# Routing the last group by token slot and loading expert blocks in two parts

## The chip, the cores and the metric

The kernel is one launch on one NeuronCore of a Trainium2 chip. It is written in Bass with the Tile framework: the source fixes what each engine does, a scheduler in the framework puts the instructions of each engine into one fixed sequence, and from then on every engine works through its own queue in order and waits on semaphores. The metric is the time of an execution on the device, in microseconds (us). The engines are called PE (TensorE), DVE (VectorE), ACT (ScalarE), POOL (GpSimd) and SP (SyncE, which here only issues DMAs).

## What is computed

2048 tokens with 256 features pass through four layers in fp32. Each layer adds a cross attention over a context of 77 positions and then a feed-forward part to the token. The change touches layer 3 alone, which is a multi-head cross attention followed by a mixture of eight experts, of which each token takes one. An expert has room for 320 tokens; tokens that find no room go to a shared overflow expert.

```python
def layer3(x, ...):
    x = x + _L3_xattn_ref(_layernorm(x), ctx_1024, Wq, Wk, Wv, Wo, rel_pos_bias, mask)
    xf = _layernorm(x)
    eid = jnp.argmax(jax.nn.softmax(xf @ router_w + router_b, axis=-1), axis=-1)
    onehot = jax.nn.one_hot(eid, 8)
    rank = jnp.cumsum(onehot, axis=0)[jnp.arange(2048), eid] - 1
    valid = rank < 320
    buf = zeros((8, 320, 256)).at[eid, where(valid, rank, 0)].add(xf * valid)
    h = relu(einsum('ecd,edh->ech', buf, w1) + b1)
    y = einsum('ech,ehd->ecd', h, w2) + b2
    yov = relu(xf @ ow1 + ob1) @ ow2 + ob2
    return x + where(valid, y[eid, rank], yov)
```

## The kernel before

**Tokens.** The tokens lie in SBUF as G = 4 groups of J = 4 slots with 128 tokens each (one per partition). A token's row has ROW = 513 floats: x (columns 0 to 255, `xs`), the normalised x (256 to 511, `xns`) and the token's number. Three helpers normalise a group: `measure` takes the statistics (BATCH_NORM_STATS2 and AGGREGATE on DVE, L147 and L148, for each slot) and rstd (two instructions on POOL, L149 and L150, for the four slots at once); `normalize` (L156, DVE) writes `xns`, a slot at a time; `turned` transposes the group on PE (L175) and copies it out of PSUM by ACT (L179) and DVE (L181). `small_logits` (L194) makes the router's logits, two small matmuls for each slot. The tiles of statistics come from a ring of three buffers, which the attention and the routing share.

**Attention of layer 3** (L862 to L998). Sixteen iterations, one for each slot of each group, run through a software pipeline: in step s, stage k works on iteration s - k. The stages are `ahead` (in a group's first three slots, the next group's `measure`, `normalize` and transposes), `queries` (L910, matmuls into a `pq` tile; rope by DVE and POOL, L769 to L779), `queries_turned` (L929), `scores` (L945, two `psc` tiles; then the softmax: L952, L959, L965, L966 on DVE, L961 on ACT, L967 on POOL), `values` (L980 transposes, L982 and L985 copies, L987 matmuls, L990 the add into x on DVE). The stages `measured`, `logits` and `send` of the routing follow behind; they are wrapped by `after`, which runs them for a group when its last slot is through. `pq`, `psc` and later `ph` share a PSUM ring of two buffers, `pbig`.

**Routing** (L1024 to L1119). `measured` takes a group's statistics, `logits` normalises, transposes and computes the logits (bias added at L1058). `send` turns them into the row of a buffer in DRAM: the largest logit (L224 to L228), the rank of a token among those of its expert (a triangular matmul L1075, a running count over the groups L1076), the overflow's rank in the same way (L1098, L1099), and the target row `to` (L1113). Then POOL issues four indirect DMAs (L1115), one for each slot, which scatter the group's 513-float rows into `buf`. A group's ranks need the counts of the groups before it.

**Experts** (L1121 to L1236). Nine blocks, the overflow block o0 with 512 rows first and then the eight experts with 320 rows each, pass through `load`, `hidden` and `answer`, each a step behind the one before. `load` brings a block's rows from `buf` by DMAs that SP issues (L1128 for the full tiles of 128 rows, L1132 for the last 64 rows), and the bias row b2 (L1134); it transposes the normalised columns on PE (L1140), copies them by ACT and DVE (L1145, L1147), converts the token numbers (L1151) and adds b2 to x on POOL (L1153). `hidden` is the first matmul (L1164, `ph`) with the relu on ACT and DVE in turn, `answer` the second (L1176, `poe`), the add of x on DVE (L1180) and the indirect store of the tokens' results by POOL (L1181). SP also issues the weights of the experts (L1210, L1212) in the same queue.

Of the kernel before, what the change touches and what calls it, by code (L numbers as in the profile page):

```python
# [22 lines left out]
F32 = mybir.dt.float32  # L23
# [5 lines left out]
ALU = mybir.AluOpType  # L29
# [4 lines left out]
P = 128  # L34
D = 256
KC = D // P
NB, S = 2, 1024
NT = NB * S
G, J = 4, 4
GT = P * J  # L40
# [3 lines left out]
E = 8  # L44
# [5 lines left out]
EPS = 1e-5  # L50
# [5 lines left out]
ROW = 2 * D + 1  # L56
# [10 lines left out]
def tile_layers(ctx: ExitStack, tc: tile.TileContext, a: dict, out: bass.AP):  # L67
    nc = tc.nc
# [4 lines left out]
    work = ctx.enter_context(tc.tile_pool(name="work", bufs=2))  # L73
    st = ctx.enter_context(tc.tile_pool(name="st", bufs=3))
# [6 lines left out]
    def pbig(name):  # L81
        return ps2.tile([P, 2, 512], F32, tag="p2", name=name)
# [20 lines left out]
    ident = cst[:, C_ID : C_ID + P]  # L103

    tokens = [xp.tile([P, J, ROW], F32, name=f"x{g}") for g in range(G)]
    xs = [t[:, :, :D] for t in tokens]
    xns = [t[:, :, D : 2 * D] for t in tokens]
# [13 lines left out]
    neghalf = cp.tile([P, J], F32, name="neghalf")  # L121
# [124 lines left out]
    def pipelined(n, *stages):  # L246

        for step in range(n + len(stages) - 1):
            for k, stage in enumerate(stages):
                if 0 <= step - k < n:  # L250
                    stage(step - k)
# [613 lines left out]
    def layer3_attention(route, wq, mb3, kblk, vds):  # L865
        with tc.tile_pool(name="a3", bufs=2) as ap, tc.tile_pool(name="a3c", bufs=1) as c3:
# [8 lines left out]
            for b, vd in enumerate(vds):  # L875
                vw = c3.tile([P, NC3, D], F32, name=f"vw3{b}")
                full = (NC3 - 1) * P
# [4 lines left out]
                vws.append(vw)  # L882
            rel = a["relbias"]
            xnTs, rbs, qTs, ss = {}, {}, {}, {}

            def transpose(g):
                xnTs[g] = turned(g, f"a3{g}")
# [107 lines left out]

            for f in begin:
                f(0)
            pipelined(G * J, ahead, queries, queries_turned, scores, values, *map(after, route))  # L998

    NSLOT = E * CAP
    buf = dp.tile([NSLOT + NT, ROW], F32, name="buf")
# [20 lines left out]
    def layer3_ffn():  # L1024
        rw = cp.tile([P, KC, E], F32, name="rw3")
# [22 lines left out]
        made = {}  # L1048

        def measured(g):  # L1050
            measure(g, f"f3{g}")

        def logits(g):
            n = f"f3{g}"
            normalize(g)
            pl = small_logits(turned(g, n), rw, n)
            made[g] = lg = st.tile([P, J, E], F32, tag="lg", name=f"lg_{n}")
            nc.vector.tensor_tensor(lg, pl, rb.unsqueeze(1).to_broadcast([P, J, E]), ALU.add)  # L1058

        def before(dst, src):  # L1060

# [59 lines left out]
        def experts():  # L1121
            outs = iter(dram_disjoint_views(out, E * 3 + 16))

            def load(n, fp, row0, rows, b2):
                m = -(-rows // P)
                xe = fp.tile([P, 4, ROW], F32, tag="xe", name=f"xe_{n}")
                full = rows // P
                nc.sync.dma_start(  # L1128
                    xe[:, :full], buf[row0 : row0 + full * P, :].rearrange("(m p) d -> p m d", p=P)
                )  # L1130
                if full < m:
                    nc.sync.dma_start(xe[: rows - full * P, full], buf[row0 + full * P : row0 + rows, :])  # L1132
                bt = fp.tile([P, D], F32, tag="b2", name=f"b2_{n}")
                nc.sync.dma_start(bt, b2.partition_broadcast(P))  # L1134
                parts = [(i, min(P, rows - i * P)) for i in range(m)]
                xT = fp.tile([P, KC, GT], F32, tag="xT3", name=f"xT_{n}")
                for c in range(KC):
                    px = pone(f"px_{n}{c}")
                    for i, w in parts:
                        nc.tensor.transpose(  # L1140
                            px[:, i * P : i * P + w], xe[:w, i, D + c * P : D + (c + 1) * P],
                            ident[:w, :w],
                        )
                    if c == 0:
                        nc.scalar.copy(xT[:, c, :rows], px[:, :rows])  # L1145
                    else:
                        nc.vector.tensor_copy(xT[:, c, :rows], px[:, :rows])  # L1147
                to = fp.tile([P, 4], U32, tag="ids", name=f"ids_{n}")
                for lo, hi, w in ((0, full, P), (full, m, rows - full * P)):
                    if lo < hi:  # L1150
                        nc.vector.tensor_copy(to[:w, lo:hi], xe[:w, lo:hi, 2 * D])  # L1151

                        nc.gpsimd.tensor_tensor(  # L1153
                            xe[:w, lo:hi, :D], xe[:w, lo:hi, :D],
                            bt[:w].unsqueeze(1).to_broadcast([w, hi - lo, D]), ALU.add,
                        )
                return xe, xT, to, parts, rows
# [29 lines left out]
            with tc.tile_pool(name="f3", bufs=2) as fp:  # L1187
# [15 lines left out]

                def first(k):
                    if k == 0:
                        made[k] = (ow1, ow2), load("o0", fp, NSLOT, GT, a["L3_ffn_ob2"])
                        return
                    e = k - 1
                    w1 = weight([P, KC, HID], f"w1_{e}")
                    nc.sync.dma_start(w1, a["L3_ffn_w1"][e].rearrange("(c p) n -> p c n", p=P))  # L1210
                    w2 = weight([P, NH, D], f"w2_{e}")
                    nc.sync.dma_start(w2, a["L3_ffn_w2"][e].rearrange("(c p) n -> p c n", p=P))  # L1212
                    made[k] = (w1, w2), load(f"e{e}", fp, e * CAP, CAP, a["L3_ffn_b2"][e])
# [21 lines left out]
                        hT = hidden(f"o{i}", fp, xT, rows, ow1, E)  # L1235
                        answer(f"o{i}", fp, hT, ow2, xe, to, parts)  # L1236

        return (measured, logits, send), experts

    with tc.tile_pool(name="masks", bufs=1) as mp:  # L1240
        mask0 = mp.tile([P, G, J * L], a["mask0"].dtype, name="mask0")
# [117 lines left out]
```

## Time and profile before

| | us |
|---|---|
| three runs | 1182.38, 1182.4, 1190.85 |
| median | 1182.4 |
| the profiled execution | 1185.39 |
| its span | 1183.5 |

| stretch of the span | from | to |
|---|---|---|
| end of layer 2's feed-forward part, last `down` add | | about 726 |
| attention of layer 3, first L910 to last L990 | 723.5 | 931.9 |
| routing of the last group, to the issue of the last scatter | 931.9 | 958.0 |
| first block's DMA issued, first `ph` matmul | 960.9 | 968.9 |
| experts | 968.9 | end |

The groups of instructions of layer 3 that cost most, from the page: L987 on PE 76.9 us in 320 instructions (380 ns each), L1176 90.3 us in 384, L1164 75.4 us in 256, L910 57.9 us in 128; L961 on ACT 67.1 us in 256. The mean clock granted to PE over the span was 0.937 of full speed.

A row of the timeline has the start, the time, the engine, the line, the operation, its output and inputs by their names, shape and count, and in brackets the idle time of the engine before it and what ended it. A clock of 1.00 means full speed.

### The profile page before, as it was taken

To read this page: it belongs to the slowest core of one execution; us is meant where nothing else is said; L and a number is where in the kernel's file an instruction comes from. 1 tells how busy PE (TensorE), PEld (TensorE's weight loads), DVE (VectorE), ACT (ScalarE), POOL (GpSimd) and SP (SyncE) were. 2 spreads that over 40 slices of the span, in tenths; PEclk is the share of its full clock that TensorE was granted. 3 is DMA by queue.
4 is the path that set the end of the run, shared out by engine and by line. 5 is a ranking of instruction groups with operands and counts; after the bars stand their busy time and mean duration, and the time that the engine had idled before them with its cause. 6 is when DMAs were issued, how large, how long until landed. Compare 5 with 4: busy or idle time off the path is not lost. (4 is left out here: it accounts for less than half of the span.)

```text
span 1183.5 us, 13880 instructions
## 1 busy us (share of the span) xinstructions
PE 1053.2 (89%) x4778; PEld 662.2 (56%) x4778; DVE 719.0 (61%) x1850; ACT 361.4 (31%) x1108; POOL 389.9 (33%) x370
## 2 busy tenths in 40 slices
PE   5699989999999879696988999999999649999996
PEld 3255544444455446354654655778788527667664
DVE  6778855775779967758686638767878311212211
ACT  1466620000567622231211010655457101101100
POOL 6443310014334324604040002765676331221221
PEclk9799998999999966698989999999999759999998
DMA  8500037432200012201020014222224120443430
GB/s 260 81 1 2 2 63 133 79 63 30 71 2 1 1 38 92 66 1 35 1 43 1 0 53 158 65 56 53 78 44 115 45 103 28 127 146 121 145 99 13
DMA packets 96951, 74.36 MB, mean 63 GB/s; under 512 B 57650, under 2 KB 84578, under 8 KB 96878
## 3 DMA queue, kind: packets, MB, share of 16 engines
q1 hardware_dynamic: 89582, 57.68, 17.8%
q10 hardware_dynamic: 4800, 9.46, 4.4%
q0 software_dynamic: 2496, 6.31, 1.5%
q8 instruction: 40, 0.66, 0.2%
q14 instruction: 33, 0.27, 0.1%
HBM read 54.83 MB, written 19.64 MB: 63 GB/s over the span
## 5 line engine op out<-in xcount | busy, mean ns | idle before, releaser
L408 ACT ACTIVATE s_a<-psc_a,mx_a 128x77 f32<-128x77 f32 x512 | 121.9, 337 | 63.6 <-DVE mx_a L406 61.4
L415 POOL TENSOR_TENSOR s_a<-s_a,sm_a 128x616 f32<-128x616 f32 x64 | 78.5, 1228 | 129.5 <-DVE sm_a L414 98.6
L537 PE MATMUL pe_f<-ew,xnT_f 128*128 128x512 f32 x256 | 117.2, 608 | 0.0
L1176 PE MATMUL poe_e<-w,hT_e 128*128 128x256 f32 (+1 forms) x384 | 90.3, 386 | 1.1 <-DVE ye_e L1180 1.1
L543 DVE SCALAR_TENSOR_TENSOR x<-pe_f,gate_f,x 128x256 f32<-128x256 f32 x128 | 61.8, 483 | 43.6 <-PE pe_f L537 40.9
L961 ACT ACTIVATE s_a<-s_a,mx_a 128x77 f32<-128x77 f32 x256 | 67.1, 347 | 48.5 <-DVE mx_a L959 48.5
L537 PEld LDWEIGHTS pe_f<-ew,xnT_f 128*128 128x128 f32 x256 | 48.3, 194 | 55.4 <-issue 53.5
L746 PE MATMUL po_f<-down2T,hT_f 128*128 128x256 f32 x256 | 68.2, 414 | 12.2 <-DVE x L753 12.0
L1176 PEld LDWEIGHTS poe_e<-w,hT_e 128*128 128x128 f32 (+1 forms) x384 | 66.0, 175 | 21.4 <-issue 2.4
L987 PE MATMUL po_a<-vw,PT_a 128*128 128x256 f32 (+1 forms) x320 | 76.9, 380 | 0.5 <-ACT PT_a L982 0.5
L1164 PE MATMUL ph_e<-xT_e,w 128*128 128x320 f32 x256 | 75.4, 438 | 0.2
L149 POOL TENSOR_SCALAR rstd_a<-mv_a 128x4 f32<-128x4 f32 x16 | 3.7, 236 | 201.2 <-DVE mv_a L148 199.7
L406 DVE TENSOR_REDUCE mx_a<-psc_a 128x4 f32<-128x308 f32 x128 | 57.8, 464 | 13.8 <-PE psc_a L397 8.2
L746 PEld LDWEIGHTS po_f<-down2T,hT_f 128*128 128x128 f32 x256 | 50.2, 205 | 26.9 <-DVE x L753 18.7
L733 PE MATMUL pgu_f<-xnT_f,gate2T 128*128 128x512 f32 x128 | 62.6, 611 | 2.1 <-DVE hT_f L739 1.9
L753 DVE SCALAR_TENSOR_TENSOR x<-po_f,cw_f,x 128x256 f32<-128x256 f32 x128 | 60.3, 478 | 6.2 <-PE po_f L746 3.7
L446 PE MATMUL pc_a<-PT_a,vblk_a 128*32 128x256 f32 (+1 forms) x512 | 57.9, 397 | 4.4 <-DVE PT_a L441 3.8
L987 PEld LDWEIGHTS po_a<-vw,PT_a 128*128 128x128 f32 (+1 forms) x320 | 57.5, 190 | 7.2 <-ACT PT_a L982 0.7
L733 PE MATMUL pgu_f<-xnT_f,up2T 128*128 128x512 f32 x128 | 60.1, 592 | 0.0
L433 PE MATMUL pPT_a<-cst,s_a 128*128 128x128 f32 (+1 forms) x320 | 56.9, 292 | 3.0 <-ACT PT_a L439 1.6
L1164 PEld LDWEIGHTS ph_e<-xT_e,w 128*128 128x128 f32 x256 | 47.4, 190 | 21.0 <-issue 2.7
L413 DVE TENSOR_REDUCE sm_a<-s_a 128x8 f32<-128x616 f32 x64 | 50.3, 786 | 14.6 <-ACT s_a L408 12.2
(290 smaller groups left out, 1954.5 us busy)
## 6 DMA issues: line engine op xcount, KB each, us to landing
w<-in_L_ffn_w SPq DMA_DIRECT2D x16, 1024.0 KB
rb_a<-in_relbias SPq DMA_DIRECT2D x16, 616.0 KB
buf<-none ACTq DMA_DIRECT2D x12, 769.5 KB
xe_e<-buf SPq DMA_DIRECT2D x8, 513.0 KB
vd<-vo SPq DMA_DIRECT2D x8, 308.0 KB
vw<-vd SPq DMA_DIRECT2D x2, 1152.0 KB
x<-in_x SPq DMA_DIRECT2D x4, 512.0 KB
ew<-in_L_ffn_expert_w SPq DMA_DIRECT2D x4, 512.0 KB
```

What stands on the lines that cost most here:

```text
L408: nc.scalar.activation(s[:, c, 4 * i + h, :], sv[:, h, :], AF.Exp, bias=mx[:, h : h + 1], scale=-1.0,)
L415: nc.gpsimd.tensor_tensor(s[:, c], s[:, c], bc(sm, L), ALU.mult)
L446: nc.tensor.matmul(pc[cols, c, :], vblk[g // 2][: wide(m), c, m, cols], t[: wide(m), m, :], start=(k == 0), stop=(k == 1),)
L537: nc.tensor.matmul(pe[:, i, :], xnT[:, kc, j * P : (j + 1) * P], ew[half][:, kc, i * 512 : (i + 1) * 512], start=(kc == 0), stop=(kc == KC ...
L543: nc.vector.scalar_tensor_tensor(x, pe[:, e // 2, (e % 2) * D : (e % 2) * D + D], gate[:, j, 4 * half + e : 4 * half + e + 1], x, ALU.mult ...
L733: nc.tensor.matmul(pgu[:, i, :], wgu[i][:, kc, e * INTER : (e + 1) * INTER], xnTs[g][:, kc, :], start=(kc == 0), stop=(kc == KC - 1),)
L746: nc.tensor.matmul(po[:, e // 2, (e % 2) * D : (e % 2) * D + D], hTs[g, half][:, e, j * P : (j + 1) * P], wd[:, 4 * half + e, :], start=Tr ...
L753: nc.vector.scalar_tensor_tensor(x, po[:, e // 2, (e % 2) * D : (e % 2) * D + D], cws[g][:, j, ee : ee + 1], x, ALU.mult, ALU.add,)
L961: nc.scalar.activation(sh[:, h, :], sh[:, h, :], AF.Exp, bias=mx[:, h : h + 1], scale=-1.0)
L987: nc.tensor.matmul(po, t[:w, m, :], vws[g // 2][:w, m, :], start=(m == 0), stop=(m == NC3 - 1))
L1164: nc.tensor.matmul(ph[:, h % 2, :rows], w1[:, kc, h * P : (h + 1) * P], xT[:, kc, :rows], start=(kc == 0), stop=(kc == KC - 1),)
L1176: nc.tensor.matmul(po, hT[:, h, i * P : i * P + w], w2[:, h, :], start=(h == 0), stop=(h == NH - 1),)
```

## The change

There are three edits in layer 3.

The first moves the stages of the routing. In groups 0 to 2 `measured` no longer has a stage of its own: it runs in the stage of `values` of the group's last slot, and `logits` and `send` each come one step earlier for it.

The second takes group 3 by slots: behind `values` of each of its slots, the new `slot_logits` takes that slot's statistics, rstd (128x1), normalises it, transposes it into a tile of the `pbig` ring, copies it by ACT, makes its logits in the other half of the same tile and adds the bias. `send` is left as it was for the group as a whole.

The third splits the block DMAs of `load` by columns: the normalised x and the token's number (257 floats) first, then x (256 floats). For the block o0 the first part is issued as four DMAs of 128 rows each. An expert's block so has four DMAs instead of two, o0 has five instead of one.

```diff
@@ layer3_attention
+            measured, logits, slot_logits, send = route
...
-            pipelined(G * J, ahead, queries, queries_turned, scores, values, *map(after, route))
+            def last(it):
+                values(it)
+                if it % J == J - 1 and it // J < G - 1:
+                    measured(it // J)
+
+            def slot_then(it):
+                if it // J == G - 1:
+                    slot_logits(it % J)
+                elif it % J == J - 1:
+                    logits(it // J)
+
+            pipelined(G * J, ahead, queries, queries_turned, scores, last, slot_then, after(send))
@@ layer3_ffn
+        def slot_logits(j):
+            g = G - 1
+            n = f"f3{g}{j}"
+            if j == 0:
+                made[g] = st.tile([P, J, E], F32, tag="lg", name=f"lg_f3{g}")
+                made["xnT"] = work.tile([P, KC, GT], F32, tag="xnT", name=f"xnT_f3{g}")
+            x, xn = xs[g][:, j, :], xns[g][:, j, :]
+            bns = st.tile([P, 6], F32, tag="bns1", name=f"bns_{n}")
+            mv = st.tile([P, 2], F32, tag="mv1", name=f"mv_{n}")
+            rstd = st.tile([P, 1], F32, tag="rstd1", name=f"rstd_{n}")
+            nc.vector.bn_stats(bns, x)
+            nc.vector.bn_aggr(mv, bns)
+            nc.gpsimd.tensor_scalar(rstd, mv[:, 1:2], EPS, None, ALU.add)
+            nc.gpsimd.tensor_tensor(rstd, rstd, neghalf[:, :1], ALU.pow)
+            nc.vector.tensor_scalar(xn, x, mv[:, 0:1], rstd, ALU.subtract, ALU.mult)
+            pt = pbig(f"pxs_{n}")
+            for c in range(KC):
+                nc.tensor.transpose(
+                    pt[:, 0, c * P : (c + 1) * P], xn[:, c * P : (c + 1) * P], ident
+                )
+            xnT = made["xnT"][:, :, j * P : (j + 1) * P]
+            nc.scalar.copy(xnT, pt[:, 0, : KC * P].rearrange("p (c q) -> p c q", q=P))
+            for kc in range(KC):
+                nc.tensor.matmul(
+                    pt[:, 1, :E], xnT[:, kc, :], rw[:, kc, :],
+                    start=(kc == 0), stop=(kc == KC - 1),
+                )
+            nc.vector.tensor_tensor(made[g][:, j, :], pt[:, 1, :E], rb, ALU.add)
@@ experts
-            def load(n, fp, row0, rows, b2):
+            def load(n, fp, row0, rows, b2, first=False):
...
-                nc.sync.dma_start(
-                    xe[:, :full], buf[row0 : row0 + full * P, :].rearrange("(m p) d -> p m d", p=P)
-                )
-                if full < m:
-                    nc.sync.dma_start(xe[: rows - full * P, full], buf[row0 + full * P : row0 + rows, :])
+
+                for cols, step in ((slice(D, ROW), 1 if first else 4), (slice(0, D), 4)):
+                    for i in range(0, full, step):
+                        r = slice(row0 + i * P, row0 + min(full, i + step) * P)
+                        nc.sync.dma_start(
+                            xe[:, i : min(full, i + step), cols],
+                            buf[r, cols].rearrange("(m p) d -> p m d", p=P),
+                        )
+                    if full < m:
+                        nc.sync.dma_start(
+                            xe[: rows - full * P, full, cols],
+                            buf[row0 + full * P : row0 + rows, cols],
+                        )
...
-                        made[k] = (ow1, ow2), load("o0", fp, NSLOT, GT, a["L3_ffn_ob2"])
+                        made[k] = (ow1, ow2), load("o0", fp, NSLOT, GT, a["L3_ffn_ob2"], True)
```

## The prediction

> **What bounds the kernel now**
>
> I read the page first (busy shares, then the forty slices), then the timeline of the region that the change touches (700 to 1180 us), then busy time by window, then TensorE's row of the expert loop beside SyncE's.
>
> ```profile
> PE 1053.2 (89%) x4778; PEld 662.2 (56%) x4778; DVE 719.0 (61%) x1850; ACT 361.4 (31%) x1108; POOL 389.9 (33%) x370
> ...
> PE   5699989999999879696988999999999649999996
> ```
>
> TensorE is busy 89% of the span; in the slices of layer 3 (from about 740 us) it stands at nine tenths but for the slices at 915 to 976 us. The windows say what they are:
>
> ```profile
> 735.00:931.90 196.90, 191.72 (x1068) 154.62 (x1068) 146.43 (x312) 107.39 (x342) 124.73 (x95) 1.00 0.27 67
> 931.90:966.60 34.70, 8.72 (x34) 7.30 (x34) 6.42 (x32) 0.58 (x1) 10.46 (x16) 0.54 0.30 108
> 966.60:1180.00 213.40, 197.07 (x792) 138.49 (x792) 40.40 (x90) 23.60 (x45) 43.95 (x45) 0.97 0.30 97
> ```
>
> The columns are length, busy PE, PEld, DVE, ACT, POOL, clock, DMA share, GB/s. The attention is TensorE's (191.7 of 196.9). Between it and the experts lie 34.7 us in which no engine is busy for even a third: a serial chain, and the largest hole in layer 3. In order:
>
> ```profile
> 931.46 0.42 DVE L990 TENSOR_TENSOR x<-x,po_a 128x256 f32<-128x256 f32 x1 [2.52 <-PE po_a L987]
> ...
> 936.75 0.96 POOL L1115 DMA_INDIRECT buf<-x,to_f  x1 [0.30 <-issue]
> 937.74 0.25 POOL L149 TENSOR_SCALAR rstd_f<-mv_f 128x4 f32<-128x4 f32 x1
> 938.07 1.04 POOL L150 TENSOR_TENSOR rstd_f<-rstd_f,neghalf 128x4 f32<-128x4 f32 x1
> 939.15 1.38 DVE L156 TENSOR_SCALAR x<-x,mv_f,rstd_f 128x256 f32<-128x256 f32 x4 [6.50 <-POOL rstd_f L150]
> ...
> 943.64 3.58 PE L194 MATMUL pl_f<-rw,xnT_f 128*128 128x8 f32 x16 [0.78 <-DVE xnT_f L181]
> 947.26 0.19 DVE L1058 TENSOR_TENSOR lg_f<-pl_f,r_L_ffn_router_b 128x32 f32<-128x32 f32 x1 [3.68 <-PE pl_f L194]
> ...
> 953.06 1.12 POOL L1115 DMA_INDIRECT buf<-x,to_f  x1 [1.36 <-DVE to_f L1113]
> ...
> 960.90 0.38 SPq L1128 DMA_DIRECT2D xe_o<-buf  x1
> ...
> 966.70 1.94 PE L1140 MATMUL px_o<-cst,xe_o 128*128 128x128 f32 x8 [13.48 <-DMA xe_o<-buf]
> ```
>
> From the last residual add (end 931.88) to the last group's first scatter 21.2 us pass: POOL does group 2's four scatters first (to 937.7), then rstd, normalise, transposes, 16 router matmuls at a halved clock, and 5.8 us of `send` from the logits to the scatter. Then 7.8 us to the first load's issue, 5.8 us to its landing, 2.2 us to the first `ph` matmul (968.85).
>
> In the expert loop TensorE waits for each block; two of the seven rows:
>
> ```profile
> 1028.35 0.66 PE L1140 MATMUL px_e<-cst,xe_e 128*128 128x128 f32 x4 [1.51 <-DMA xe_e<-buf]
> ...
> 1053.16 0.63 PE L1140 MATMUL px_e<-cst,xe_e 128*128 128x128 f32 x4 [2.22 <-DMA xe_e<-buf]
> ```
>
> The seven idle times (timeline of TensorE, 1007 to 1143 us) are 0.44, 1.51, 2.22, 0.63, 1.90, 0.46, 1.84: 9.0 us.
>
> **The change, part by part**
>
> All against the profiled execution (1185.39 us, span 1183.5), 3.0 above the median 1182.4.
>
> *A. Start of attention 3.* By the compiled order, group 3's measure and normalise leave the end of layer 2's FFN and the attention's start: the three-buffer ring of statistics turns differently. Gone from there are four BATCH_NORM_STATS2/AGGREGATE pairs (0.60 each, between `down` adds that TensorE waits 0.15 to 0.19 us for, in a cycle of 4.33 us) and one normalise of 3.40 us (729.54 to 732.94) in front of the second rope (732.86). TensorE then waits in 735 to 740 us (1.05 us on POOL at 737.75, 0.51 and 0.23 on DVE r_a), and the next `pq` starts at 740.22. With the ropes 3.4 us earlier these waits go: 1.8, and some 0.3 from the `down` cycle. **-2.1**; bounds -2.6 (all) and -0.5 (only the `down` cycle, other queues catch up).
>
> *B. Middle of the attention.* The same 2.4 us of statistics and 1.4 us of normalise (0.35 each, the row at 939.15) reappear on DVE, and 1.3 us (L149 and L150) on POOL, at iterations 4 to 6. DVE is busy 146.4 of 196.9 us there, TensorE's idle rows are only 1.96, 0.63 and 0.29 us. Cover: DVE's free quarter. Bounds: 0 (all hidden) and +3.8 (all on the path); the windows put it near 0. **+1.0**.
>
> *C. Last group by slot.* TensorE's work is the same in count (8 transposes, 8 small matmul pairs), but slots 0 to 2 go between attention matmuls at full clock, and only slot 3's remain behind the last add. New waits, from the compiled order: the slot's tile comes from the two-buffer PSUM ring that `pq` and `psc` use, so iteration 15's second `psc` half stands behind slot 0's bias add, on DVE behind slot 1's normalise, which waits for POOL's rstd. Queued behind it on TensorE is `values`(14), behind that `values`(15), for which POOL's scaling (L967) and all else wait. I walked TensorE through the tail with the row durations: an added stall of 1.2 us near 910, the scaled softmax of iteration 15 at about 930.6 instead of 920.6, last `po` at 936.3 instead of 931.4. On POOL group 2's four scatters (0.96 and 0.30 each, 5 us, now about 930.7 to 935.6) stand before slot 2's rstd; on DVE slot 2's normalise stands before the last add. So that add ends near 937.5, **5.6 us later than today**. Behind it: statistics 0.6, rstd 1.4, normalise 0.4, two transposes 0.6, ACT copy 0.45, four matmul rows 0.9 (0.22 each, as at 943.64), add 0.25, together 4.6; then `send` 5.8: scatter at 947.9 against 953.06. **-5.2**; bounds -7 (no tail stall) and 0 (tail stall twice as long).
>
> *D. First block in parts.* Today 1026 KB land 5.76 us after issue, the next 513 KB 1.66 us later: 317 GB/s, so 1026 KB take 3.3 us and 2.45 are fixed, and the fixed part of the second lay beside the first. Four pieces of 128 KB, issued 0.45 apart (the issues at 960.90 and 961.33), last issue +1.35, last landing about +4.2 (1.35 + 2.45 + 0.4). All but two transposes are done by then; +0.45 and a copy of 0.6 give the first `ph` at +5.3 instead of +7.95. **-2.65**. Against this speaks the Trainium skill, page "DMA: Bandwidth & Descriptors", section "Measured (HBM→SBUF, 128 partitions, SWDGE, issued from GpSimd)": "Batch DMAs to ≥1 MiB for ≥75% of peak. Transfers under 64 KB are descriptor-dominated." Its table has 0.95 us for 64 KB and 6.15 for 1 MB; four pieces of 128 KB, read between (an estimate, 1.3 each) and put one after the other, take 5.2 us: -0.9 instead of -2.65, and the whole sum -12.1 instead of -13.8. I take the row, since it shows two transfers from this buffer overlapping. Bounds -3 and 0.
>
> *E. Experts in parts.* The transposes need only the normalised half and the id: 257 KB instead of 513 before the wait ends, 257 KB / 317 GB/s = 0.83 us earlier. Against the seven waits: 0.44 + 0.83 + 0.83 + 0.63 + 0.83 + 0.46 + 0.83 = **-4.85**. Rows become 1 KB long. The trace has 1-KB rows: a 1-MB w2 load ahead of the block moves its landing from 4.26 us after issue (1002.87 to 1007.13) to 6.9 (1091.83 to 1098.76), 2.67 us per MB, no slower. Bounds -9.0 (waits vanish) and +1 (fixed cost decides, and one more issue of 0.47 ahead in the queue). Costed at nothing: two more issues on SyncE per expert (0.94 us; b2 and w go out that much later, but w1 issued at 1011.52 is first used after 1033); POOL's bias add (L1153) waits for the second part, but its consumer `answer` comes a whole `hidden` (some 20 us) later.
>
> *The `send` of groups 0 to 2 a stage earlier*: 24 small DVE rows near 0.2 us each; they move within the attention, under TensorE's cover: 0, at most +1 where a scatter (5 us of POOL per group) delays an L967.
>
> Sum: -2.1 + 1.0 - 5.2 - 2.65 - 4.85 = -13.8; 1171.6 on the profile's own time, **1168.6 against the median**.
>
> **Rivals**
>
> *1. The split brings nothing in the loop.* If the wait is latency (2.45 of the 4.26 us are fixed) and not bytes, E is about 0 and D is -0.9: -7.2, **1175**. For it: the fixed part is the larger one. Against: landings spread by bytes (1.66 us for 513 KB).
>
> *2. The attention does not start earlier, and its middle pays.* A -0.5, B +3.8: -9.4, **1173**. For: layer 2's cycle is TensorE's own anyway. Against: the 1.05 us wait at 737.75 is on a POOL rope that waited for DVE.
>
> *3. Slower: the in-order tail.* Each slot's transposes wait on TensorE for their normalise, with the attention's matmuls queued behind them, while the tile holds half of the ring. The round trip add, statistics, rstd behind an L967 (1.2), normalise, transposes, copy, matmuls, add is 4.6 to 5 us; four slots uncovered and 5 us of scatters make 25 us, 19.4 more than C has: +5.6, **1188**. For: the compiled order has these waits. Against: the order puts other matmuls (16 to 20 `po` of 3.6 to 4.5 us) between most of them. It decides from the point where the last residual add ends later than 951 us (937.5 + 13.8); below that the kernel is faster.
>
> *That it doesn't do what it says* is excluded by the order: the moves are there.
>
> **How the numbers follow**
>
> Forecast 0.55, rival 1 0.22, rival 2 0.13, rival 3 0.10. A measurement here tells from no change about 1%, 11.8 us: faster means below 1170.6, slower above 1194.2. The forecast's own spread (D, E and C have bounds of 2 to 5 us each, about 4 together) puts 0.7 of it below 1170.6: 0.39; of the rivals 1 and 2, whose terms can also come out larger, 0.13. Faster 0.52. Rival 3 reaches 1194 in half its cases with D and E also lost: 0.06. The rest, 0.42, lies within 1%. The range leaves out rival 3's upper part and a tenth at the low end (all terms at their better bounds would be 1158): 1160 to 1182.
>
> **What would show it**
>
> A: the first `pq` after the first scores near 738, the L156 of 3.40 us gone from 729. C: the last L990 near 935 (937.5 less A and B), one L1115 group ahead of it, the last group's first scatter 10 us behind. D: first px_o transposes 4 us or less after the issue, `ph` 5.3 after it. E: px_e waits of 0 to 1.4 us, together about 4. Wrong: px_e waits as today (rival 1), TensorE's busy share of the attention below 95% before 900 us (rival 2), or an L990 beyond 951 (rival 3).

## The result, and the profile after

The changed kernel takes 1179.1 us (median of 15 runs, 1172.23 to 1185.37) beside 1187.07 us for the kernel before in the same series (15 runs, 1182.24 to 1192.16): ratio 0.9933, 95% interval 0.991 to 0.9956. That is 8 us, 0.7%, where 13.8 us were forecast. Its profiled execution took 1182.58 us with a span of 1180.8.

The layers before layer 3 have the same instructions in both kernels, and yet their gate matmuls end at 706.1 us in the profile before and at 710.1 in the profile after; over all runs of this study that point lies between 704.4 and 715.1. The forecast is therefore checked by stretches that begin after it. Each is the difference of two times in the timeline of TensorE, DVE, POOL or SyncE, in one profiled execution of each kernel.

| stretch, us | before | after | difference | forecast |
|---|---|---|---|---|
| end of layer 2's gate matmuls to the fourth slot's first `pq` (before: 740.22) | 34.13 | 31.89 | -2.24 | A -2.1 |
| from there to the transposes that wait for POOL in group 3 (before: 902.13) | 161.91 | 167.99 | +6.08 | B +1.0, send 0 |
| from there to the last group's first scatter | 50.93 | 43.81 | -7.12 | C -5.2 |
| first scatter to the issue of the first load | 7.84 | 8.28 | +0.44 | 0 |
| first load to the first `ph` | 7.95 | 5.24 | -2.71 | D -2.65 |
| first `ph` to expert 0's first `ph` | 25.39 | 26.45 | +1.06 | 0 |
| from there to the last `poe` | 179.89 | 177.56 | -2.33 | E -4.85 |
| sum | 468.04 | 461.22 | -6.82 | -13.8 |

First the kernel after in windows from the fourth slot's `pq` to the last add, from there to the first block's transposes, and the experts. The columns are the same as before: length, busy PE, PEld, DVE, ACT, POOL, clock, DMA share, GB/s.

```profile
742.00:943.70 201.70, 191.59 (x1060) 152.92 (x1058) 154.75 (x325) 105.85 (x340) 129.29 (x106) 1.00 0.27 66
943.70:964.30 20.60, 5.09 (x22) 4.11 (x21) 4.78 (x27) 0.74 (x2) 5.92 (x12) 0.54 0.23 77
964.30:1177.00 212.70, 196.98 (x792) 137.00 (x792) 39.86 (x90) 23.57 (x45) 43.94 (x45) 0.97 0.33 103
```

The hole between attention and experts is 14 us shorter (20.6 for 34.7). But the attention is longer, and TensorE is idle for 10.1 of its 201.7 us, where it was idle for 3.5 of 191.7 before. So part of the gain is paid back ahead of the hole. The chain through the hole, from the timeline after:

```profile
941.03 0.96 POOL L1157 DMA_INDIRECT buf<-x,to_f  x1 [0.30 <-issue]
...
943.29 0.42 DVE L991 TENSOR_TENSOR x<-x,po_a 128x256 f32<-128x256 f32 x1
...
945.37 0.41 DVE L1087 TENSOR_SCALAR x<-x,mv_f,rstd_f 128x256 f32<-128x256 f32 x1
...
948.11 0.17 DVE L1100 TENSOR_TENSOR lg_f<-pxs_f,r_L_ffn_router_b 128x8 f32<-128x8 f32 x1 [2.33 <-PE pxs_f L1096]
...
953.81 1.12 POOL L1157 DMA_INDIRECT buf<-x,to_f  x1 [1.36 <-DVE to_f L1155]
...
962.09 2.23 SPq L1174 DMA_DIRECT2D xe_o<-buf  x5
964.28 0.29 PEld L1190 LDWEIGHTS px_o<-cst,xe_o 128*128 128x128 f32 x2 [10.40 <-issue]
964.31 1.63 PE L1190 MATMUL px_o<-cst,xe_o 128*128 128x128 f32 x6 [10.34 <-DMA xe_o<-buf]
```

Group 2's scatters now end before the last add, and behind it only one slot is routed: 10.1 us from the end of the add to the first scatter, where 21.2 were needed. The first block's transposes begin 2.2 us after the first issue, for 5.8 before. In the expert loop (TensorE after) the waits are not gone:

```profile
1026.79 0.66 PE L1190 MATMUL px_e<-cst,xe_e 128*128 128x128 f32 x4 [1.78 <-DMA xe_e<-buf]
...
1064.46 5.89 PE L1214 MATMUL ph_e<-xT_e,w 128*128 128x320 f32 x20
1071.63 0.66 PE L1190 MATMUL px_e<-cst,xe_e 128*128 128x128 f32 x4 [1.28 <-DMA xe_e<-buf]
```

They sum to 8.8 us, for 9.0 before. The next rows come from the middle of the attention after, where the 6 us are lost. They show two of the places where TensorE waits for DVE, with the DVE and POOL rows ahead of them.

```profile
820.01 2.35 POOL L779 TENSOR_TENSOR q_a<-q_a,r_a 128x1024 f32<-128x1024 f32 x1 [0.94 <-DVE sm_a L967]
820.35 2.06 DVE L225 TENSOR_TENSOR hot_f<-lg_f,lmx_f 128x32 f32<-128x32 f32 x1
...
824.33 0.28 PE L1117 MATMUL pr_f<-tot_f,cst 128*128 128x8 f32 x1 [0.89 <-DVE tot_f L1115]
...
838.30 2.38 DVE L1148 SCALAR_TENSOR_TENSOR os_f<-os_f,pov_f,o_f 128x4 f32<-128x4 f32 x1
838.32 2.34 POOL L779 TENSOR_TENSOR q_a<-q_a,r_a 128x1024 f32<-128x1024 f32 x1
...
840.73 0.44 PE L175 MATMUL pxnT_a<-cst,x 128*128 128x128 f32 x2 [1.73 <-DVE os_f L1148]
```

Instructions on four or 32 numbers per partition, which take about 0.2 us in the tail, take 2.1 and 2.4 us here, and both end within 0.05 us of POOL's rope addition that runs beside them. The kernel before has the same long rows, in its own order:

```profile
815.64 2.35 POOL L779 TENSOR_TENSOR q_a<-q_a,r_a 128x1024 f32<-128x1024 f32 x1
815.99 2.05 DVE L225 TENSOR_TENSOR hot_f<-lg_f,lmx_f 128x32 f32<-128x32 f32 x1
...
819.69 0.20 DVE L1073 TENSOR_REDUCE tot_f<-hot_f 128x8 f32<-128x32 f32 x1
...
832.58 0.28 PE L1075 MATMUL pr_f<-tot_f,cst 128*128 128x8 f32 x2
...
843.02 2.39 DVE L1106 SCALAR_TENSOR_TENSOR os_f<-os_f,pov_f,o_f 128x4 f32<-128x4 f32 x1
```

Between the two points of the table's second row, the 42 DVE rows of the routing last 16.0 us in sum before and 17.9 after, so the long rows are hardly new. What is new is who waits. TensorE took the counts `tot_f` 12.7 us after they were ready before, and at once after. TensorE has the same 864 instructions there in both kernels. Of the 6.1 us, 4.7 are more idle time, and 1.4 are longer rows, for which no cause was found. Ahead of the wait at its end the stretch has five waits of over half a microsecond after, of 0.84, 0.89, 1.50, 1.73 and 1.53 us, where there was one of 1.96 before. The second and the fourth of them are the two shown; the first stands behind the normalise of 4.88 us (803.59), and the 1.50 and 1.53 are for ACT's copies of the transposed weights of the softmax (`PT_a`). By the starts of the `pq`, the kernel after is 0.2 us late at the tenth and 5.9 at the twelfth and at the last. So nearly the whole loss lies beside group 0's routing, and next to none beside group 1's.

### The profile page after: what moved, and what is told of

It is laid out like the page before. It is cut to its first block, busy times and chain, and to the rows that moved or that the text cites. A ratio compares the mean times of both kernels' runs of the same rounds, so it can differ in the third digit from the quotient of the medians.

```text
span 1180.8 us, 13922 instructions
## 1 busy us (share of the span) xinstructions
PE 1058.2 (90%) x4778; PEld 664.2 (56%) x4778; DVE 722.2 (61%) x1852; ACT 362.7 (31%) x1111; POOL 391.8 (33%) x376
## 5 line engine op out<-in xcount | busy, mean ns | idle before, releaser
L746 PEld LDWEIGHTS po_f<-down2T,hT_f 128*128 128x128 f32 x256 | 50.4, 206 | 26.5 <-DVE x L753 18.3
L1056 ACT ACTIVATE hT_e<-ph_e,b1c 128x320 f32<-128x320 f32 (+1 forms) x36 | 19.6, 545 | 136.6 <-PE ph_e L1214 136.6
L1058 DVE TENSOR_SCALAR hT_e<-ph_e,b1c 128x320 f32<-128x320 f32 (+1 forms) x36 | 20.6, 573 | 64.8 <-PE ph_e L1214 64.8
L739 DVE TENSOR_TENSOR hT_f<-sg_f,pgu_f 128x512 f32<-128x512 f32 x32 | 22.0, 686 | 61.8 <-ACT sg_f L738 61.8
```

The source lines that it names most:

```text
L746: nc.tensor.matmul(po[:, e // 2, (e % 2) * D : (e % 2) * D + D], hTs[g, half][:, e, j * P : (j + 1) * P], wd[:, 4 * half + e, :], start=Tr ...
```

## The experiments

All ratios are against the kernel before, run on the same chip in the same series. Where a text speaks of the third `pq`, the point meant is the fourth slot's first `pq`, from which 161.9 us pass before and 168.0 after to the transposes that wait for POOL. In the table the stretches are those from above: routing is from the end of layer 2's gate matmuls to the last group's first scatter.

| run | ratio (95%) | to fourth `pq` | `pq` to POOL's wait | to scatter (routing) | load to `ph` | `ph` to e0 | experts |
|---|---|---|---|---|---|---|---|
| before | 1 | 34.1 | 161.9 | 247.0 | 7.95 | 25.4 | 179.9 |
| after | 0.9933 | 31.9 | 168.0 | 243.7 | 5.24 | 26.5 | 177.6 |
| e1 split only | 0.9945 (0.9922 to 0.9968) | 34.1 | 162.3 | 247.4 | 5.31 | 26.2 | 176.9 |
| e2 routing only | 0.9966 (0.9943 to 0.9989) | 31.9 | 167.0 | 242.5 | 7.92 | 25.7 | 180.7 |
| e3 slots late | 0.993 (0.9908 to 0.9953) | 34.1 | 161.9 | 248.7 | 4.74 | 25.6 | 177.7 |
| e4 xe three buffers | 0.9875 (0.9824 to 0.9926) | 31.9 | 168.4 | 244.0 | 5.49 | 25.5 | 173.3 |
| e5 ring of four | 0.989 (0.9857 to 0.9923) | 31.9 | 168.0 | 243.7 | 5.15 | 26.7 | 176.3 |
| e6 mixed | 0.9888 (0.9853 to 0.9923) | 34.1 | 162.6 | 240.6 | 5.43 | 26.3 | 177.0 |
| e8 mixed, xe three | 0.9844 (0.9808 to 0.9879) | 34.1 | 162.0 | 240.0 | 5.18 | 26.7 | 173.3 |
| e9 statistics early | 0.9853 (0.9809 to 0.9897) | 31.9 | 162.8 | 237.8 | 5.27 | 26.0 | 173.3 |

### The two halves alone: e1 and e2

e1 is the kernel before with the new `load` only, e2 the changed kernel with the old `load` (L1128 to L1132 as before).

> Only the block DMAs in two parts, on the kernel before; routing as before. By the account of the two traces (first block -1.65 us after 1.06 us of colder matmuls, experts -2.3 us) this run is 4 us faster than the kernel before (ratio 0.9966), the seven waits of the expert transposes still sum to about 8.8 us, and the first ph comes about 5.2 us after the first load's issue. By the prediction's own terms D and E it would be 7.5 us faster (0.9937) with waits of about 4 us in sum.

> Only the routing edits, block DMAs as before. By the account of the two traces (attention start -2.2, its middle +6.1, from there to the last group's first scatter -7.1) this run is about 3 us faster than the kernel before (ratio 0.9973). By the prediction (A -2.1, B +1.0, C -5.2) it would be 6.3 us faster (0.9947). The first scatter of the last group comes about 213.6 us after the first scores' third pq matmul, before 212.8.

The split alone gives 6.5 us by the runs (between the two expectations, and its interval holds both), and 3.5 by the stretches of its one profile; the waits of the transposes sum to 8.0 us and the first `ph` comes 5.3 us after the first load. The routing alone gives 4.0 us, between 3 and 6.3 as well; its first scatter comes 210.6 us after the fourth slot's `pq` (212.8 before), 3 us earlier than the account gave. Both halves gain, and the loss in the middle (167.0) belongs to the routing.

### Which part of the routing costs the middle: e3, e5, e6, e9

e3 puts the stages of groups 0 to 2 back:

```diff
-            pipelined(G * J, ahead, queries, queries_turned, scores, last, slot_then, after(send))
+            def measure_then(it):
+                if it // J == G - 1:
+                    slot_logits(it % J)
+                elif it % J == J - 1:
+                    measured(it // J)
+            def logits_then(it):
+                if it % J == J - 1 and it // J < G - 1:
+                    logits(it // J)
+            pipelined(G * J, ahead, queries, queries_turned, scores, values, measure_then, logits_then, after(send))
```

> The changed kernel with the stages of groups 0 to 2 put back as before (measured, logits and send each a stage later); the last group still goes by slots and blocks still load in two parts. If the moved stages of groups 0 to 2 cause the 6 us lost in the attention's middle, these come back, the gain of 2.2 us at its start goes, and the run is about 11 us faster than the kernel before (ratio 0.991). If the loss comes from the slots themselves (their statistics, rstd and tiles), the ratio stays at 0.9933 or gets worse by the lost start (0.995), and the middle still loses 4 to 6 us.

The middle is as before (161.9), so the slots do not cost it; the moved stages do. But the forecast gain of 11 us was a miss: with group 2 routed late, its `send` and scatters fall beside the slots, and POOL's wait to the first scatter takes 52.6 us instead of 43.8. The early stage is needed for group 2.

e5 was to test the prediction's reason for the moved normalise, the ring of statistics (the tiles mv and rstd likewise, and the tile sel in two buffers to make room):

```diff
-        stats = st.tile([P, J, 6], F32, tag=f"bns{kind}", name=f"bns_{name}")
+        stats = st.tile([P, J, 6], F32, tag=f"bns{kind}", name=f"bns_{name}", bufs=3 if kind else 4)
...
```

> The changed kernel with four buffers instead of three for the statistics that attention and routing share (and two instead of three for the tile sel, to make room), so that group 3's statistics and its normalise go back to the end of layer 2. If the turned ring is what loses time in the attention's middle, the loss of 6.1 us there falls to 1 to 2 us, the gain of 2.2 us at the start goes, and the run is 2 us faster than the changed kernel (0.9915). If it is the earlier logits and send of groups 0 and 1, whose short DVE instructions are held up, only the stall of 0.84 us behind the normalise goes, 4 to 5 us stay lost, and the run is equal to the changed kernel or up to 2 us slower (0.994 or more).

All stretches of the routing are those of the changed kernel to 0.1 us, the stall of 0.83 us behind the normalise among them. So the number of buffers in the ring is not the reason. (Its ratio is better than the changed kernel's, but the intervals overlap, and in the stretches only the experts differ, by 1.3 us.)

e6 routes group 2 in the new stages, and groups 0 and 1 in the old ones (statistics in the next stage, logits and send one later each):

```diff
             def last(it):
                 values(it)
-                if it % J == J - 1 and it // J < G - 1:
+                if it % J == J - 1 and it // J == G - 2:
                     measured(it // J)
...
```

> The changed kernel with groups 0 and 1 routed in the stages of the kernel before, and only group 2 a stage earlier; the last group by slots, blocks in parts. If the earlier stages of groups 0 and 1 cost the middle, the POOL wait of the transposes at 168 us after the third pq comes back to 162 us as before, the tail stays as short as in the changed kernel (43.8 us from there to the last group's first scatter), and the run is about 4 us faster than the changed kernel although the start's 2.2 us are gone (0.990 against the kernel before). If the short tail of the changed kernel needs the early stages of all groups, the tail is longer by 5 us or more and nothing is gained (0.994).

It came out as the first theory said: 162.6, then 43.8 us to the first scatter, and a ratio of 0.9888. The stalls behind `tot_f` and `os_f` are gone. The early routing of groups 0 and 1 costs the middle.

e9 is the same with three buffers for `xe` (see e8), and only the statistics of groups 0 and 1 early.

```diff
-                if early(it):
+                if early(it) or late(it):
                     measured(it // J)
...
```

> The kernel of e8_mixed_xe3, but with the statistics of groups 0 and 1 taken in the stage of their last values as in the changed kernel; their logits and send stay in the stages of the kernel before. If taking group 0's statistics earlier is what moves group 3's statistics and normalise out of the start, the first pq of the fourth slot comes 31.9 us after the end of layer 2's gate matmuls (34.1 in e8), the stall of 0.84 us behind the long normalise is back near 68 us, and the stalls at 82 and 99 us (0.89 and 1.73) are absent; the run is 1 to 2 us faster than e8 (0.983). If the earlier logits and send did that, start and middle are as in e8 (0.9844).

The start is that of the changed kernel (31.9), a stall of 0.77 us behind the long normalise is back at 67.9 us, and the stalls at 82 and 99 us are absent. So the early statistics bring term A, at a price below 1 us, and the early `logits` and `send` of groups 0 and 1 cost 5.2 us (168.0 against 162.8). The time of the run is not told apart from e8's (0.9853 against 0.9844, each with 0.4% on either side); the 2 us stand in the stretches only.

### Why short DVE instructions got long: e7 and e10

Behind the experts of the changed kernel, DVE forms run alone and beside an addition of two 128x1024 tensors on POOL (the code is e10's, shortened):

```diff
+        for k in range(8):
+            nc.scalar.copy(pa, pc)
+            if k % 2:
+                nc.gpsimd.tensor_tensor(pd, pa, pc, ALU.add)
+            nc.vector.tensor_reduce(pm, pa[:, :512], AX.X, ALU.add)
+            if k // 2 == 0:
+                nc.vector.scalar_tensor_tensor(s3[:, :32], s1[:, :32], pm[:, 0:1], s2[:, :32], ALU.add, ALU.mult)
+            elif k // 2 == 1:
+                nc.vector.scalar_tensor_tensor(s3[:, :32], pq[:, :32], pm[:, 0:1], s2[:, :32], ALU.add, ALU.mult)
...
```

> The changed kernel with a measurement of single instructions behind it: each DVE form once alone and once while POOL adds two 128x1024 tensors in SBUF (2.4 us). If DVE is held up where both of its inputs lie in SBUF, or where a tensor_scalar reads and writes SBUF, the 128x32 product of two SBUF tensors takes 0.2 us alone and 1.5 us or more beside POOL, ending with POOL's instruction, and so does the tensor_scalar from SBUF; the product with one input in PSUM, the tensor_scalar from PSUM, the reduction and the statistics take the same in both cases. If the long rows are only waits of the profile for other reasons (data, the queue), all forms take the same in both cases. The time of the run itself is some 20 us longer than the changed kernel.

> As e7_port, with the two-tensor forms made to follow the reduction, so that they begin while POOL's addition runs. If DVE is held up where both tensor inputs lie in SBUF, the scalar_tensor_tensor and the tensor_tensor on 128x32 take 0.2 us alone and about 1.5 us beside POOL, ending with POOL's instruction; the same two forms with one input in PSUM take 0.2 us in both cases. If two inputs in SBUF make no difference, all stay at 0.2 us.

In e7 the two-tensor products ran before POOL began, so that run left them open; e10 answers it. Timeline of e10 (pb_s and pb_t lie in SBUF, pb_p in PSUM), first alone, then beside POOL, then the same form with PSUM beside POOL:

```profile
1173.11 0.25 DVE L1356 SCALAR_TENSOR_TENSOR pb_u<-pb_s,pb_m,pb_t 128x32 f32<-128x32 f32 x1
...
1174.84 2.34 POOL L1353 TENSOR_TENSOR pb_d<-pb_a,pb_c 128x1024 f32<-128x1024 f32 x1 [3.14 <-ACT pb_a L1351]
1175.44 1.78 DVE L1356 SCALAR_TENSOR_TENSOR pb_u<-pb_s,pb_m,pb_t 128x32 f32<-128x32 f32 x1
...
1181.11 2.34 POOL L1353 TENSOR_TENSOR pb_d<-pb_a,pb_c 128x1024 f32<-128x1024 f32 x1 [3.93 <-ACT pb_a L1351]
1181.72 0.25 DVE L1360 SCALAR_TENSOR_TENSOR pb_u<-pb_p,pb_m,pb_t 128x32 f32<-128x32 f32 x1
```

The second row ends at 1177.22, POOL's at 1177.18. With a PSUM input nothing is added. The tensor_tensor goes from 0.19 to 1.77 us, and stays at 0.19 with PSUM. The form of the normalise, timeline of e7:

```profile
1192.19 0.35 DVE L1360 TENSOR_SCALAR pb_u<-pb_s,pb_m 128x256 f32<-128x256 f32 x1
...
1194.01 2.34 POOL L1353 TENSOR_TENSOR pb_d<-pb_a,pb_c 128x1024 f32<-128x1024 f32 x1 [3.85 <-ACT pb_a L1351]
1194.62 1.88 DVE L1360 TENSOR_SCALAR pb_u<-pb_s,pb_m 128x256 f32<-128x256 f32 x1
```

From PSUM it takes 0.48 in both cases, a reduction of 32 numbers 0.18 and the statistics 0.42. This is what the Trainium skill says on its page "SBUF — State Buffer", section "Who interferes with whom": a DVE instruction with two SBUF inputs, or in the two-port mode that a tensor_scalar can enter, and a GpSimd instruction that reads SBUF exclude each other for the whole instruction. The trace agrees to 0.1 us.

A held row need not cost anything, though. In e9 the row of L1148 (there L1166) is held as long, but TensorE works on:

```profile
850.45 2.40 DVE L1166 SCALAR_TENSOR_TENSOR os_f<-os_f,pov_f,o_f 128x4 f32<-128x4 f32 x1
850.45 2.37 POOL L779 TENSOR_TENSOR q_a<-q_a,r_a 128x1024 f32<-128x1024 f32 x1
851.87 0.60 PE L930 MATMUL pqT_a3t<-cst,q_a 128*128 128x128 f32 x4
```

In the changed kernel the transposes `pxnT_a` of the next group stand right behind it, and they take the single PSUM buffer (`pside`) that `pov_f` holds until L1148 has read it.

### What the expert loop waits for: e4 and e8

```diff
-                xe = fp.tile([P, 4, ROW], F32, tag="xe", name=f"xe_{n}")
+                xe = fp.tile([P, 4, ROW], F32, tag="xe", name=f"xe_{n}", bufs=3)
```

> The changed kernel with three buffers instead of two for the tile xe of a block, so that a block's load no longer waits for the answers of the block two before. If the wait of the expert transposes is a matter of when the load can be issued, the seven waits (8.8 us) go to under 1 us and the run is 8 us faster than the changed kernel (0.9865 against the kernel before). If it is a matter of transfer or of the fixed cost of DMAs, they stay and the ratio is 0.992 or more.

> The kernel of the run e6_mixed with three buffers for the tile xe as in e4_xe3. If the two gains lie in different stages and add up, it is 4 us faster than e4_xe3 and about 8 us faster than e6_mixed (0.984 against the kernel before); if they overlap, it is no better than e4_xe3 (0.9875).

All waits of the transposes are gone, and from expert 0's first `ph` to the end TensorE is busy for 173.1 of 173.3 us. With two buffers a load is issued only when the answers of the block two before have been added. The stretch is 4.3 us shorter, not 8.8: TensorE is busy for 4.9 us more there with the same 705 instructions. In the trace it goes over from `ph` to `poe` 45 times instead of 25, most transposes stand 0.20 us apart instead of 0.11, and more `poe` rows 0.31 instead of 0.22; why the pace changes with the order stays open. The ratio goes from 0.9933 to 0.9875, but the two intervals overlap, so the gain is shown by the stretch. With the routing of e6 (e8) both gains add up in the stretches.

The stretch of the experts holds one more thing than waits. In the profile before, the granted clock is 0.50 for 3.41 us (1053.91 to 1057.33), right behind the longest of the seven waits, 2.22 us. The first of these two rows lies there, the second, of the same form, at a clock of 1.00:

```profile
1053.62 5.31 PE L1176 MATMUL poe_e<-w,hT_e 128*128 128x256 f32 x16
...
1099.22 3.62 PE L1176 MATMUL poe_e<-w,hT_e 128*128 128x256 f32 x16
```

That is 1.7 us. e2, with the old `load`, has such a stretch as well (1057.29 to 1060.70), behind a wait of 2.32 us, and no run with the split has one. Whether the shorter waits prevent it was not tested.

### The clock behind the hole: e11 to e15

e11 adds 18 matmuls that nobody reads to e8; e12 has 9 on e9 (its edit is shown). e13 and e14 are e9 without and with the 9, and expert 0's transposes behind the first eight `ph` matmuls. The profile has two rows for each of these matmuls, so that is behind sixteen rows; in e9 itself they stand behind eight rows, and not before the `ph`, as the text of e13 has it. e15 is e14 with expert 0's number conversion behind the first block's copy on DVE.

```diff
+                wt = fp.tile([P, P], F32, tag="warm", name="warm", bufs=1)
+                nc.vector.tensor_scalar(wt, ident, over[:, 0:1], None, ALU.mult)
+                pw = pbig("pwarm")
+                for i in range(9):
+                    nc.tensor.matmul(pw[:, i % 2], wt, ow1[:, 0, :512], start=True, stop=True)
```

> The kernel of e8_mixed_xe3 with 18 matmuls of 128x512 that nobody reads on TensorE between the last count and the first block's transposes, while it would wait for the scatter and the load. If the slow first ph matmuls (6.4 us for eight instead of 3.6) come from the clock after the idle stretch, the stretch from the first ph to expert 0's first falls from 26.7 us to about 24.4 and the run is 2 us faster than e8 (0.9827). If they wait for something else, it stays at 26.7 (0.9844); if the matmuls hold up the first transposes, it gets longer.

> The kernel of e9_measure_early with 9 unread matmuls instead of the 18 of e11_warm, so that they end before the first block lands: in e11 they ran 18.2 us and held up the first transposes by 7 us, while the stretch behind them was 3.1 us shorter. If the clock is what made the first ph matmuls slow, the transposes start 2.2 to 2.6 us after the first load's issue as in e8, the stretch from the first ph to expert 0's first is about 23.5 us instead of 26, and the run is 3 to 4 us faster than e9 (0.982 against the kernel before). If the gain of e11's short stretch came only from the blocks having landed meanwhile, it stays at 26 and the ratio at 0.985.

> The kernel of e9_measure_early with expert 0's block transposes queued on TensorE behind the first eight ph matmuls of the overflow block, where the changed kernel has them, instead of before them. No unread matmuls. The stretch from the last group's first scatter to the first ph falls by about 0.3 us; the first eight ph still run at half clock (about 6.3 us) and the run is equal to e9 within 1 us (0.985).

> e13_order with the 9 unread matmuls of e12_best. If the clock after the idle stretch is what step D lost, the first eight ph take about 3.7 us instead of 6.3, first ph to expert 0's first is about 23.5 us instead of 26, and the time from the first scatter to expert 0's first is about 3 us shorter than in e13_order (ratio about 0.982). If the first ph are slow for another reason (the late DVE half of the copy, their PSUM tile), both stretches are as in e13_order.

> e14_order_warm with expert 0's token numbers converted on DVE behind the overflow block's copy, as in e13_order; in e14 they stood before it and held the second ph matmuls up by 3.4 us. Now only the 9 unread matmuls differ from e13_order. If the clock is what step D lost, the stretch from the first ph to expert 0's first is about 23.5 to 24.5 us (26.9 in e13_order) and the run is 2 to 3 us faster than e13_order (0.981). If not, it is equal to e13_order (0.983).

e11: ratio 0.9859 (0.9814 to 0.9903). The matmuls ran 18.2 us and held the first transposes up by 7 us, and the stretch behind was 23.5 us. e12: 0.9855 (0.9821 to 0.989), inconclusive: TensorE waited 3.2 us for expert 0's transposes ahead of the first `ph`, and the clock fell again (0.50 at 966 to 970 us). e14: 0.9884 (0.9849 to 0.9919), spoilt by a DVE order that held the `ph` up for 3.4 us. In the order around the first `ph`, e13 and e15 differ in the unread matmuls alone. TensorE in e13, without:

```profile
959.48 2.05 PE L1209 MATMUL px_o<-cst,xe_o 128*128 128x128 f32 x8 [10.54 <-DMA xe_o<-buf]
962.03 9.90 PE L1233 MATMUL ph_e<-xT_o,ow 128*128 128x512 f32 x16 [0.51 <-ACT xT_o L1214]
```

and in e15, with:

```profile
952.07 10.35 PE L1273 MATMUL pwarm<-ow,warm 128*128 128x512 f32 x18
962.76 1.84 PE L1209 MATMUL px_o<-cst,xe_o 128*128 128x128 f32 x8 [0.34 <-DMA xe_o<-buf]
965.21 7.32 PE L1236 MATMUL ph_e<-xT_o,ow 128*128 128x512 f32 x16 [0.61 <-ACT xT_o L1214]
```

The same sixteen rows take 7.3 us instead of 9.9; the granted clock is 0.56 in e13's first 6 us of `ph` and 1.00 in e15's. First `ph` to expert 0 takes 24.3 us instead of 26.9. In the runs e13 has 0.9833 (0.9792 to 0.9873) and e15 0.9839 (0.9803 to 0.9876): the 2.6 us of the profile can't be told at this spread. The fastest versions found are e8, e9, e11, e12, e13 and e15 (0.983 to 0.986, with intervals that overlap); their order stays open.

## Why the prediction was right or wrong

- **The serial hole as the place of the gain: right.** C was forecast at -5.2 and is -7.1. The last add came 4.0 us later in its own stretch, for 5.6 forecast, and the add to the scatter fell from 21.2 to 10.1 us, for 10.4 forecast. The feared wait of `psc` and the scatters cost less than walked.
- **A: right in size (-2.2 for -2.1), wrong in its reason.** Not the number of buffers in the ring (e5) but the place of groups 0 and 1's statistics brings it (e9).
- **B and "the `send` of groups 0 to 2 a stage earlier: 0, at most +1": the step that failed.** The middle lost 6.1 us. The prediction said "24 small DVE rows near 0.2 us each; they move within the attention, under TensorE's cover". By e9 against the changed kernel the early logits and `send` of groups 0 and 1 account for 5.2 us of it; the early statistics cost 0.8 (e9 against e8). Two things were missed. A row of 0.2 us lasts up to 2.4 where POOL adds two SBUF tensors beside it (e10), and the kernel before showed such rows already (L225, 2.05 us at 815.99, and L1106, 2.39 us at 843.02). And TensorE's cover ended: these rows lasted about as long before, but in the changed kernel TensorE's queue had the counts and the next group's transposes right behind them. Term B priced group 3's normalise at 0.35 us a slot, though the row of 3.40 us that term A counted was the same normalise; it came back at 4.9 us for four slots. The stalls that the trace puts right behind held rows of the routing, 0.89 and 1.73 us, are half of the 5.2; how the rest divides between held rows and the mere place of the work was not separated.
- **D: the term was right at its place (-2.71 for -2.65), and part was given back behind it.** The granted clock is 0.50 until 971.99 us before and until 972.70 after, and the first `ph` begins at 968.85 before and at 967.33 after. So the `ph` run at half the clock for 3.1 us before and for 5.4 after; 2.2 us more at half the pace are 1.1 us, an estimate from these times, beside the 1.06 that the stretch lost. e15 against e13 shows that this clock is worth 2.6 us of the stretch where all of it is removed. The prediction took the matmuls behind the landing at an unchanged length. It was right to trust the row against the rule that it weighed: four pieces of 128 KB did not take their time one after the other. The first transposes began 2.2 us after the first issue, and those of the last piece 4.05 us after it, for 4.2 forecast.
- **E: mis-sized, -2.3 for -4.85, and what came is not what was forecast.** The forecast was for the waits of the transposes, and they fell by 0.2 us in sum. Blocks that were waited for in both kernels landed 0.2 to 0.9 us sooner after their issue, 0.5 in the mean of six, for 0.83 worked out from bytes. But the sum subtracted that from waits of a fixed order. The order after has the transposes of three blocks behind 20 instead of 24 `ph` rows, so that TensorE arrives 1.1 us sooner. In these three the waits grew from 2.6 to 4.4 us, and in the other four they fell from 6.4 to 4.4. What ends the wait is the issue, which hangs on the buffers of `xe` (e4). Most of the 2.3 us, 1.7, is the stretch of half clock in the profile before, which only the two kernels with the old `load` show.
- **First scatter to first load:** 7.84 us before, 8.0 to 9.7 in every other run but none with a cause found; 0.4 us of the miss.
- **A sum:** all terms at their better bounds give -21.6 us and so 1160.8 us; the prediction has 1158.

Rival 1 (no gain from the split) was the nearest to the measured time. Its sign came, transposes that wait as today (8.8 us for 9.0), but not its reason: the landings did follow the bytes in part, and D was -2.71 where it had -0.9. Rival 2 named the right stretch, the middle, but charged it to group 3's statistics and normalise, of which e9 shows 0.8 us, and A was not lost. Its sign did not come: TensorE is busy for 151.1 of the 158.0 us from 742 to 900 us, 95.6%. Rival 3 did not occur: the last add ended at 943.7 us, in a profile that was 4 us late from the layers before.

## What to carry to other kernels

When short VectorE instructions are moved into a stage where GpSimd adds tensors in SBUF, price each with two SBUF inputs at the remaining length of the GpSimd instruction. Then look at what TensorE has queued behind its reader, above all where a PSUM ring has one buffer: here the long rows were there before as well, and TensorE waited only where its own work stood right behind them. When a wait for a transfer is to be shortened, ask first what its issue waits for: here one more buffer removed all of it, and halving the bytes hardly any. After an idle stretch, count the first matmuls at the clock that the profile grants there.

## What was not expected of the hardware

The exclusion between DVE and POOL is complete to 0.1 us: a 128x32 instruction of 0.19 us took 1.77 us, and with one input in PSUM it took 0.19 beside the same POOL addition. TensorE's clock rose 5.0 us after the unread matmuls began in e11 (946.2 to 951.2 us; their rows stand 0.85 us apart ahead of this and 0.43 behind it), 4.8 us after their begin in e15 and 3.2 in e12. In e12 it fell to 0.50 at 963.44 us, which is 0.5 us into the wait of 3.2 us. In the 3.41 us up to that point TensorE was busy for 1.70. In all seventeen traces of this study each stretch at one clock is a whole multiple of 3.413 us long, the first and the last of a trace aside. The Trainium skill, page "TensorE: Matmul & The Clock Gate", section "What's actually happening", gives a free-running window of 3413 ns, and these lengths agree with it. It has the slow clock follow an idle window; here it followed one in which TensorE was busy half of the time.
